# Local transformer of a twelve-stage kernel: queries scaled by their norms on GpSimd instead of the softmax exponents, with the sums of squares and the pieces of the feed-forward block moved

## The chip, the cores and the metric

The kernel runs on one core of a Trainium2 chip. The metric is the device time of one execution in microseconds; the median of three runs of the kernel before is 5602.67 us (5600.59 to 5613.93). The engines are named as in the profile: PE is TensorE's matrix multiply and PEld its weight load, DVE is VectorE, ACT is ScalarE, POOL is GpSimd, SP is SyncE, whose queue issues the DMAs here.

## The reference, cut to what matters

The reference is a chain of twelve blocks on x of 8 x 256 tokens, 128 wide. Blocks seven and nine are the same six-layer local transformer, `_L2_ffn_ref`, with the same weights; the change touches it alone. A layer of it is

```
q, k, v = split(shift_tokens(x) @ Wqkv)            # 16 heads of 64
q = l2norm(q) * q_scale ;  k = l2norm(k) * k_scale  # t / max(norm, 1e-12)
q, k = rotary with a scale for q and its inverse for k
sim  = (window of 32 queries) . (64 keys: window before and own) * 8
sim  = where(mask, -max, sim) ;  attn = softmax(sim) ;  out = attn @ v
x = out @ Wo + x
x = (a * gelu(gate)) @ W2 + b2 + x     # a, gate from layernorm(shift_tokens(x)) @ W1 + b1
```

The norm of a query is one number for each token and head. It may scale the query before the product with the keys, or the score row after it.

## The kernel before, in words

Tokens lie along the free axis in four groups of 512 (two sequences of 256), channels on the 128 partitions. The 16 heads are taken in four "quads" of four heads; in a quad's tiles of 128 x 2 x 512 the partitions hold two heads of 64 channels, and the index j holds the other two. A stage of the local transformer has 6 layers x 4 groups x 4 quads = 96 quads, so the two stages have 192.

`ffn2` (L1588) is a software pipeline written by hand. One pass of its loop, a *round*, works on four quads at once: q0 is projected, q1 gets its scores, q2 its exponentials and its product with the values, q3 is transposed back. Within these stages the calls go through `_Ordered` (L285), which ties each instruction of DVE, ACT, POOL and PE to the one issued before it on the same engine. So the order of calls in `ffn2` is the order on every engine.

What the steps of a round do:

- `quad_project` (L1315), for k and then for q: two 512-column products give `pp` in PSUM; ACT squares it into `l_sq`; DVE multiplies it by the cosines into `l_y`; DVE shuffles neighbouring partitions into `l_yr`; POOL multiplies that by the sines and adds it to `l_y`.
- `quad_norms` (L1345): four products with `hsum` add the squares of each head in one PSUM bank; ACT takes logarithm and exponential, which gives `l_rn`, the reciprocal norms times a constant, with k, q, k, q in four blocks of 32 rows; two DMAs on SP's queue bring the key rows to `l_rt`.
- `quad_pick` (L1357): eight small products with `hpick` turn the query rows of `l_rn` so that they lie as the score rows do; DVE bounds them by 1e12 into `l_rq`. Two DVE shuffles of 128 x 512 spread the rows of `l_rt` over the partitions, into a tile of the tag `l_sq`.
- `quad_keys` (L1375): one DVE scalar_tensor_tensor bounds that and multiplies the rotated keys by it, into `l_kp`.
- `quad_scores` (L1383): mask and 128 products of 64 x 32 give `sc`; DVE takes the row maximum `l_mx` and subtracts it, giving `l_e`; POOL multiplies `l_e` by `l_rq`.
- `quad_exp` (L1416): ACT's exponential of `l_e`. `quad_turn` (L1419): eight PE transposes `et`, which ACT copies to `l_at`. `quad_weigh` (L1429): 64 products in each of two halves `cx`, divided on DVE. `quad_back` and `quad_done`: eight transposes `ct`, copied by ACT to `l_ct`. `quad_values` (L1333): four products `vp`, copied by ACT to `l_v`, and two DMAs to `l_w`.

`pp`, `et`, `ct`, `cx`, `sc`, `vp` and `ge` share three PSUM tiles of two banks each. Which of them a step gets is settled when the program is built; it waits on the chip until that tile's last readers are done.

After the last quad of a group, `local_rest` (L1468) does the output projection and the feed-forward block in *pieces*; `piece` (L1583) runs the generator to its next `yield` at four places of each round. In what follows four rounds are told apart by the pieces in them. Round W: the output projection `wo_acc` in three pieces and the residual `x`, then the shifted copies `l_xs`. Round N: the layer norm, its first half (`acc`, `ln_c`, `ln_sq`) and its second (`acc`, `lv`, `ln_r`, `t`). Round G: the gated projections `ge`, `l_gl`, `l_ag` and two thirds of `w_acc`. Round X: the last third and the sum `x`. There are 48 such groups of four rounds.

Of the kernel before, what the change touches and what calls it, by code (L numbers as in the profile page):

```python
# [24 lines left out]
ALU = mybir.AluOpType  # L25
# [3 lines left out]
P = 128  # L29
B, S, D = 8, 256, 128  # L30
NB = 2
T = NB * S
# [6 lines left out]
WIN = 32  # L39
# [3 lines left out]
SH = 20.0  # L43
# [9 lines left out]
def _constants():  # L53

    f = np.float32
    p = np.arange(P)
    c = {}
    c["ident"] = np.eye(P, dtype=f)
    c["mean"] = np.full((P, P), 1.0 / P, f)
    c["ones"] = np.ones((P, P), f)  # L60
    c["iota"] = np.tile(np.arange(E, dtype=f), (P, 1))
    c["krow"] = (p % 32 == DH).astype(f)[:, None]
    c["eps"] = np.tile(
        np.array([1e-5, 2e-5, 2.0**-64, 0.5 * SH * math.log(2.0)], f), (P, 1)
    )
    blk = (p[:, None] // 64 == p[None, :] // 64).astype(f)
    c["blkm"] = blk / f(64)

    z = np.zeros((P, 32), f)
    z[:64, :16] = 1.0  # L70
    z[64:, 16:] = 1.0
    c["hsum"] = z
    z = np.zeros((P, 4), f)
    for n, r in enumerate((32, 96, 48, 112)):
        z[r, n] = 1.0
    c["hpick"] = z

    r = np.zeros((P, P), f)
    for m in range(P):
        if m % 2 == 0:  # L80
            r[m + 1, m] = -1.0
        else:
            r[m - 1, m] = 1.0
    c["rot2"] = r

    sel = np.zeros((P, 4, P), f)
    for g in range(4):
        for j in range(4):
            for d in range(DH):
                sel[DH * (4 * g + j) + d, g, 32 * j + d] = 1.0  # L90
    c["sel"] = sel.reshape(P, -1)


    lev = [np.eye(P, dtype=f)]
    for i in range(7):
        n = 2**i
        q = p // n
        lev.append(((q[:, None] % 2 == 0) & (q[None, :] == q[:, None] + 1)).astype(f))
    c["lev"] = np.concatenate(lev, 1)

    c["cq"] = np.where(p[None, :] > p[:, None], f(NEG), f(0))
    c["ck"] = np.where(p[:, None] > p[None, :], f(NEG), f(0))
    one9 = np.zeros((P, 32), f)
    one9[:, DH] = 1.0
    c["one9"] = one9


    i, key = np.arange(32), np.arange(64)
    ok = (key[None, :] >= i[:, None]) & (key[None, :] <= i[:, None] + WIN)
    m = np.zeros((2, 2, 32, 2, 64), f)  # L110
    m[:, 0] = np.where(ok, f(0), f(LNEG))[:, None, :]
    m[:, 1, :, 0, :WIN] = LNEG
    c["lmask"] = m.reshape(P, -1)
    m = np.zeros((2, 2, 32, 4, 32), f)
    m[:, 0] = np.eye(32, dtype=f)[:, None, :]
    m[:, 1, :, 0] = np.eye(32, dtype=f)
    c["lrow"] = m.reshape(P, -1)

    half = np.arange(0, 64, 2, dtype=f)
    inv_freq = f(1.0) / f(10000.0) ** (half / f(64))  # L120
    t = np.arange(S, dtype=f)
    fr = t[:, None] * inv_freq[None, :]
    fr = np.concatenate([fr, fr], -1).T
    base = (half + f(0.4 * 64)) / f(1.4 * 64)
    sc = base[None, :] ** ((t - f(S // 2)) / f(WIN // 2))[:, None]
    sc = np.concatenate([sc, sc], -1).T
    two = lambda a: np.concatenate([_partners(a.T).T] * 2, 0).astype(f)

    sgn = np.where(p[:64, None] < 32, f(-1), f(1))
    c["qcos"] = two(np.cos(fr) * sc * f(8.0))  # L130
    c["qsin"] = two(np.sin(fr) * sc * f(8.0) * sgn)
    c["kcos"] = two(np.cos(fr) * (f(1.0) / sc))
    c["ksin"] = two(np.sin(fr) * (f(1.0) / sc) * sgn)

    i = np.arange(DH // 2, dtype=f)
    th = np.power(f(10000.0), f(-2.0) * (i - f(1.0)) / f(DH))
    ang = t[:, None] * th[None, :]
    per = lambda a: np.tile(np.repeat(a.T, 2, axis=0), (NH, 1)).astype(f)
    c["rcos"] = per(np.cos(ang))
    c["rsin"] = per(np.sin(ang))  # L140

    groups = {
        "c1": ("ident", "mean", "ones", "iota", "krow", "eps"),
        "cs0": ("cq", "ck"),
        "cs1": ("lev", "blkm"),
        "cs2": ("hsum", "hpick", "lmask", "lrow", "qcos", "qsin", "kcos", "ksin"),
        "cs3": ("rot2", "sel", "ck", "one9", "rcos", "rsin"),
    }
    return {n: {k: c[k].astype(f) for k in ks} for n, ks in groups.items()}
# [159 lines left out]
class _Net:  # L309
# [1002 lines left out]
            out[k] = t.unsqueeze(1).to_broadcast([P, 4, S])  # L1312
        return out

    def quad_project(self, q, n):  # L1315

        nc = self.nc
        four = lambda a: a.rearrange("p j (b s) -> p (j b) s", b=NB)
        o = S if n == "k" else 0
        pp = self.two("pp")  # L1320
        for j in range(2):
            self.mm(pp[:, j, :], q.w[:, o + P * j : o + P * (j + 1)], q.xs)
        sq = self.work("l_sq", (P, 2, T), bufs=3)
        nc.scalar.activation(sq, pp, AF.Square)
        y = self.work("l_y" + n, (P, 2, T), bufs=2)
        nc.vector.tensor_tensor(four(y), four(pp), q.tab[n + "cos"], ALU.mult)
        yr = self.work("l_yr", (P, 2, T), bufs=2)
        nc.vector.stream_shuffle(yr, pp, [i ^ 1 for i in range(32)])
        nc.gpsimd.tensor_tensor(four(yr), four(yr), q.tab[n + "sin"], ALU.mult)
        nc.gpsimd.tensor_tensor(y, y, yr, ALU.add)  # L1330
        q.y[n], q.sq[n] = y, sq
# [10 lines left out]
        nc.sync.dma_start(w[:32, 1::2], v[96:, 0::2])  # L1342
        q.v = (w, v)

    def quad_norms(self, q):  # L1345


        nc = self.nc
        sp = self.ps()
        for s, (n, j) in enumerate((("k", 0), ("q", 0), ("k", 1), ("q", 1))):  # L1350
            self.mm(sp[32 * s : 32 * s + 32, :], self.get("hsum"), q.sq[n][:, j, :])
        q.rn = self.work("l_rn", bufs=2)
        self.rsqrt(q.rn, sp, 2, scale=2.0**SH, shift=3)
        for j in range(2):
            nc.sync.dma_start(self.rt[j::32], q.rn[64 * j : 64 * j + 32 : 8, :])

    def quad_pick(self, q):  # L1357


        nc = self.nc  # L1360
        tp = self.ps()[:, :16].rearrange("p (m r) -> p m r", r=4)
        for b in range(NB):
            for x in range(2):
                for c in range(2):
                    o = S * b + P * c + 64 * x
                    self.mm(tp[64 * c : 64 * c + 64, 2 * b + x, :], q.rn[:, o : o + 64], self.get("hpick"))
        q.rq = self.work("l_rq", (P, 16), bufs=2)
        nc.vector.tensor_scalar(
            q.rq.rearrange("p (r m) -> p r m", m=4), tp.rearrange("p m r -> p r m"), 1e12, None,
            ALU.min)  # L1370
        q.rk = self.work("l_sq", (P, 2, T), bufs=3)
        for j in range(2):
            nc.vector.stream_shuffle(q.rk[:, j, :], self.rt, [j] * 32)

    def quad_keys(self, q):  # L1375

        nc = self.nc
        q.kp = self.kp[q.n % len(self.kp)]
        nc.vector.scalar_tensor_tensor(
            q.kp[:, :, WIN:], q.rk.rearrange("p j (b s) -> p (j b) s", b=NB), 1e12,  # L1380
            q.y["k"].rearrange("p j (b s) -> p (j b) s", b=NB), ALU.min, ALU.mult)

    def quad_scores(self, q):  # L1383

        nc = self.nc
# [7 lines left out]
        for j in range(2):  # L1393
            for b in range(NB):
                for x in range(2):
                    o = S * j + P * b + 64 * x
# [9 lines left out]
        sl = lambda a: a.rearrange("p (n k) -> p n k", k=64)  # L1406
# [3 lines left out]
        nc.vector.tensor_reduce(mx, sv, AX.X, ALU.max)  # L1410
        e = self.work("l_e", (P, 2 * T), bufs=2)
        nc.vector.tensor_tensor(sl(e), sv, bc(mx), ALU.subtract)
        nc.gpsimd.tensor_tensor(sl(e), sl(e), bc(q.rq), ALU.mult)
        q.e = e

    def quad_exp(self, q):  # L1416
# [51 lines left out]
    def local_rest(self, u):  # L1468
# [5 lines left out]
        def project(cs):  # L1474
            for c in cs:
                self.mm(acc, u.w["wo"][:, c, :], u.ct[c // 2][:, c % 2, :], start=c == 0, stop=c == 7)
# [2 lines left out]
        yield False  # L1479
        project(range(3, 6))  # L1480
        yield False
        project(range(6, 8))
        u.x1 = self.new_x()
        nc.vector.tensor_tensor(u.x1, acc, self.ys[u.g], ALU.add)
        xs = self.shifted(u.x1)
        yield False

        yield False
        self.settle()
        norm = self.norm_parts(xs, gamma=self.get(f"F{i}_ln_g"), beta=self.get(f"F{i}_ln_b"),  # L1490
                               out=self.scratch("t", bufs=2), bank=self.bank1)
        next(norm)
        yield True
        yield True
        u.hn = yield from norm
# [92 lines left out]
    def ffn2(self):  # L1588
# [7 lines left out]
        while True:  # L1596
            q0 = next(gen, None)
            if not (q0 or q1 or q2 or q3 or left):
                break
            left = max(left - 1, 0)  # L1600
            if q1:
                self.quad_pick(q1)
            if q1:
                self.quad_keys(q1)
            if q0:
                self.quad_project(q0, "k")
                if not q0.n:
                    self.window_rows()
            if q2:
# [3 lines left out]
            self.piece(pieces)  # L1613
            if q2:
                self.quad_turn(q2)
            if q3:
                self.quad_back(q3)
                self.quad_done(q3)
                if q3.last:
                    pieces, left = self.local_rest(q3.unit), 4  # L1620
            if q2:
                self.quad_weigh(q2)
            self.piece(pieces, True)
            if q0:
                self.quad_norms(q0)
            self.piece(pieces)
            if q1:
                self.quad_scores(q1)
# [143 lines left out]
```

## Time and profile before

| What | Value |
|---|---|
| Median of three runs | 5602.67 us |
| Profiled execution, its own time | 5608.06 us |
| Span in its profile | 5606.2 us |
| Granted TensorE clock, mean | 0.974 |
| PE busy | 5052.7 us (90%) |
| DVE busy | 3506.1 us (63%) |
| ACT busy | 2461.2 us (44%) |
| POOL busy | 2340.9 us (42%) |
| Chain that ended last, by engine | PE 66%, DVE 20%, ACT 9%, issue 4%, POOL 1% |

Line 300 of the kernel is the helper in `_Ordered` that makes every call of the local transformer, so the groups of the profile are told apart by their tiles and not by lines. In a row "out<-in ... xN | busy, mean ns | idle before <-releaser" the last part is the idle time of the engine just before these instructions, and what ended most of it. `bank` is the one-bank tile that `hsum`'s and `hpick`'s products share with layer norms outside these stages. "issue" as a releaser means that the engine waited for nothing that the profile shows.

### The profile page before, as it was taken

What the parts mean: (1) busy time and instruction counts of PE and PEld (TensorE: products, weight loads), DVE (VectorE), ACT (ScalarE), POOL (GpSimd) and SP (SyncE); (2) the same over time, 40 slices, a digit from 0 to 9 for tenths busy, and PEclk for the clock granted to TensorE, in tenths of its full rate; (3) what the DMA queues carried; (4) which work ended last, traced back from release to release, by engine and by line L of the source; (5) the groups of instructions that cost most, each with busy time, mean ns of one, the idle gap of its engine ahead of it and who ended that gap; (6) DMA issues with size and microseconds to landing.
All of it is one profiled execution on the core that took longest, in us unless ns stands there. A gap on an engine that the chain in (4) does not pass through costs nothing.

```text
span 5606.2 us, 161762 instructions
## 1 busy us (share of the span) xinstructions
PE 5052.7 (90%) x73456; PEld 2970.4 (53%) x73456; DVE 3506.1 (63%) x5863; ACT 2461.2 (44%) x2947; POOL 2340.9 (42%) x1205
## 2 busy tenths in 40 slices
PE   9999997898999999989889899989899999899889
PEld 6755754455555555555444455555555555455446
DVE  4444446776766767676645667767667777645555
ACT  2233235444544444454434445544444554433342
POOL 0000012666665666666500666656566656501000
PEclk9999989999999999999989999999999999999899
DMA  1000000111111111111000011110111111000000
GB/s 66 1 1 1 1 1 22 30 35 37 36 40 33 39 34 41 34 35 34 26 23 1 26 38 37 35 38 28 45 30 44 31 38 34 26 34 1 1 1 8
DMA packets 58335, 149.56 MB, mean 27 GB/s; under 512 B 9649, under 2 KB 23858, under 8 KB 57394
## 3 DMA queue, kind: packets, MB, share of 16 engines
q1 hardware_dynamic: 57650, 139.21, 8.1%
q8 instruction: 578, 9.47, 0.7%
q14 instruction: 107, 0.88, 0.1%
HBM read 45.52 MB, written 1.05 MB: 8 GB/s over the span
## 4 chain that ended last, share of the span: by engine, by line
PE 66%; DVE 20%; ACT 9%; issue 4%; POOL 1%; DMA 0%; DVEq 0%; SPq 0%; ACTq 0%; POOLq 0%
PE mm L355 10%; PE bank L300 7%; PE e_o L355 6%; PE wo_acc L300 6%; PE sc L300 6%; PE pp L300 6%; PE vp L300 5%; PE ge L300 5%; DVE l_yr L300 4%; PE cx L300 4%; DVE l_yk L300 4%; PE ct L300 3%; PE ms L300 3%; DVE l_kp L300 2%; ACT l_ct L300 2%
## 5 line engine op out<-in xcount | busy, mean ns | idle before, releaser
L300 POOL TENSOR_TENSOR l_yr<-l_yr,l_ksin 128x1024 f32<-128x1024 f32 x192 | 456.2, 2376 | 1010.8 <-DVE l_yr L300 1010.8
L300 PE MATMUL pp<-l_xs,wqkv 128*128 128x512 f32 x1536 | 716.1, 609 | 5.2 <-DMA wqkv<-in_f_wqkv 3.6
L300 DVE TENSOR_REDUCE l_mx<-sc 128x16 f32<-128x1024 f32 x192 | 235.1, 1225 | 566.1 <-PE sc L300 566.1
L300 POOL TENSOR_TENSOR l_e<-l_e,l_rq 128x1024 f32<-128x1024 f32 x192 | 365.3, 1903 | 383.8 <-DVE l_e L300 357.8
L300 ACT ACTIVATE l_sq<-pp 128x1024 f32<-128x1024 f32 x384 | 391.1, 1018 | 279.6 <-PE pp L300 279.6
L300 DVE STREAM_SHUFFLE l_yr<-pp 128x1024 f32<-128x1024 f32 x384 | 505.3, 1316 | 0.0
L355 PE MATMUL mm<-x,m 128*128 128x512 f32 x1024 | 480.0, 609 | 1.2 <-ACT e_a L387 1.2
L300 ACT COPY l_v<-vp 128x1024 f32<-128x1024 f32 x192 | 194.3, 1012 | 611.8 <-PE vp L300 609.5
L300 POOL TENSOR_TENSOR l_yq<-l_yq,l_yr 128x1024 f32<-128x1024 f32 x192 | 454.9, 2369 | 15.1
L300 POOL TENSOR_TENSOR l_yk<-l_yk,l_yr 128x1024 f32<-128x1024 f32 x192 | 452.4, 2356 | 15.0
L300 POOL TENSOR_TENSOR l_yr<-l_yr,l_qsin 128x1024 f32<-128x1024 f32 x192 | 454.8, 2369 | 0.0
L300 PEld LDWEIGHTS pp<-l_xs,wqkv 128*128 128x128 f32 x1536 | 278.3, 191 | 290.3 <-issue 283.8
L300 PE MATMUL cx<-l_w,l_at 64*32 64x65 f32 x12288 | 326.2, 227 | 87.1 <-ACT l_ct L300 43.9
L355 PEld LDWEIGHTS e_o<-m,e_h 128*128 128x128 f32 x3072 | 363.0, 192 | 60.6 <-issue 60.1
L300 PE MATMUL vp<-wqkv,l_xs 128*128 128x256 f32 x1536 | 384.9, 393 | 6.2 <-issue 6.2
L355 PE MATMUL e_o<-m,e_h 128*128 128x128 f32 x3072 | 363.5, 275 | 0.0
L300 PE MATMUL wo_acc<-l_ct,wo 128*128 128x512 f32 x768 | 362.2, 605 | 0.0
L300 ACT ACTIVATE lv<-bank,sb_c 128x512 f32<-128x512 f32 x221 | 151.1, 684 | 478.0 <-PE bank L300 477.1
L300 PE MATMUL cx<-l_v,l_at 64*32 64x65 f32 x12288 | 334.1, 228 | 22.7 <-issue 22.7
L300 PEld LDWEIGHTS cx<-l_w,l_at 64*32 64x32 f32 x12288 | 259.2, 107 | 154.6 <-ACT l_ct L300 72.3
L300 PE MATMUL ct<-sb_c,l_cx 128*128 128x128 f32 x1536 | 206.6, 278 | 127.8 <-DVE l_yr L300 70.5
L300 PE MATMUL sc<-l_kp,l_yq 64*32 64x64 f32 x24576 | 297.9, 227 | 26.2 <-issue 25.5
(285 smaller groups left out, 9682.6 us busy)
## 6 DMA issues: line engine op xcount, KB each, us to landing
l_w<-l_v SPq DMA_DIRECT2D x192, 390.0 KB
wqkv<-in_f_wqkv SPq DMA_DIRECT2D x48, 384.0 KB
l_w<-l_v SPq DMA_DIRECT2D x192, 65.0 KB
wo<-in_f_wo SPq DMA_DIRECT2D x12, 512.0 KB
l_rt<-l_rn SPq DMA_DIRECT2D x384, 8.0 KB
m<-in_m_w SPq DMA_DIRECT2D x16, 256.0 KB
w<-in_f_w SPq DMA_DIRECT2D x12, 341.0 KB
w<-in_f_w SPq DMA_DIRECT2D x12, 192.0 KB
```

The source lines that it names most:

```text
L300: r = f(*args, **kw)
L355: self.nc.tensor.matmul(out, lhsT=lhsT, rhs=rhs, start=start, stop=stop)
```

## The change

`hpick`, its eight products, `l_rq` and POOL's multiplication of `l_e` are gone. Four DMAs instead of two bring the key rows and the query rows of `l_rn` to `l_rt`; four shuffles instead of two spread them. POOL bounds the queries' factors by 1e12 and multiplies the rotated queries `l_yq` by them, ahead of the scores. The tag `l_sq` has four buffers instead of three.

The order within a round changes in four places. The keys are scaled after the cosine product of the next quad's k instead of before it. The sums of squares stand between the transposes `et` and `ct` instead of after the products with the values, and their roots after the copy of `ct`. The pieces of a group begin at the first place of round W instead of the second. The first half of the layer norm stands at the first place of round N, between the projections and `quad_turn`, instead of the second place, after `quad_weigh`; the second half stays at the last place of round N, and the pieces of rounds G and X stay where they were.

```diff
-    c["hpick"] = z
...
+    def quad_project(self, q, n, q1=None):
...
+        sq = self.work("l_sq", (P, 2, T), bufs=4)
         nc.scalar.activation(sq, pp, AF.Square)
         y = self.work("l_y" + n, (P, 2, T), bufs=2)
         nc.vector.tensor_tensor(four(y), four(pp), q.tab[n + "cos"], ALU.mult)
+        if q1:
+            self.quad_keys(q1)
         yr = self.work("l_yr", (P, 2, T), bufs=2)
...
     def quad_norms(self, q):
         sp = self.ps()
         for s, (n, j) in enumerate((("k", 0), ("q", 0), ("k", 1), ("q", 1))):
             self.mm(sp[32 * s : 32 * s + 32, :], self.get("hsum"), q.sq[n][:, j, :])
+        q.sums = sp
+
+    def quad_roots(self, q):
+        nc = self.nc
         q.rn = self.work("l_rn", bufs=2)
+        self.rsqrt(q.rn, q.sums, 2, scale=2.0**SH, shift=3)
         for j in range(2):
+            for k in range(2):
+                at = 64 * j + 32 * k
+                nc.sync.dma_start(self.rt[2 * k + j :: 32], q.rn[at : at + 32 : 8, :])
+
+    def quad_spread(self, q):
+        nc = self.nc
+        q.r = {}
+        for k, n in ((1, "q"), (0, "k")):
+            r = q.r[n] = self.work("l_sq", (P, 2, T), bufs=4)
+            for j in range(2):
+                nc.vector.stream_shuffle(r[:, j, :], self.rt, [2 * k + j] * 32)
+        nc.gpsimd.tensor_scalar(q.r["q"], q.r["q"], 1e12, None, ALU.min)
+        nc.gpsimd.tensor_tensor(q.y["q"], q.y["q"], q.r["q"], ALU.mult)
...
-        nc.gpsimd.tensor_tensor(sl(e), sl(e), bc(q.rq), ALU.mult)
...                                              # local_rest
         project(range(3, 6))
         yield False
+        yield False
         project(range(6, 8))
         u.x1 = self.new_x()
         nc.vector.tensor_tensor(u.x1, acc, self.ys[u.g], ALU.add)
         xs = self.shifted(u.x1)
         yield False
 
-        yield False
         self.settle()
         norm = self.norm_parts(xs, ...)
         next(norm)
+        yield True
         yield True
         yield True
         u.hn = yield from norm
...                                              # ffn2
+            if q3 and q3.last:
+                pieces, left = self.local_rest(q3.unit), 4
             if q1:
-                self.quad_pick(q1)
-            if q1:
+                self.quad_spread(q1)
+            if q0:
+                self.quad_project(q0, "k", q1)
+            elif q1:
                 self.quad_keys(q1)
-            if q0:
-                self.quad_project(q0, "k")
...
             self.piece(pieces)
             if q2:
                 self.quad_turn(q2)
+            if q0:
+                self.quad_norms(q0)
             if q3:
                 self.quad_back(q3)
                 self.quad_done(q3)
-                if q3.last:
-                    pieces, left = self.local_rest(q3.unit), 4
+            if q0:
+                self.quad_roots(q0)
             if q2:
                 self.quad_weigh(q2)
             self.piece(pieces, True)
-            if q0:
-                self.quad_norms(q0)
             self.piece(pieces)
```

More of the change, by code (lines that the diff above doesn't have):

```diff
@@ L72, in _constants @@
     c["hsum"] = z
-    z = np.zeros((P, 4), f)
-    for n, r in enumerate((32, 96, 48, 112)):
-        z[r, n] = 1.0
-    c["hpick"] = z
     r = np.zeros((P, P), f)
@@ L145, in _constants @@
         "cs1": ("lev", "blkm"),
-        "cs2": ("hsum", "hpick", "lmask", "lrow", "qcos", "qsin", "kcos", "ksin"),
+        "cs2": ("hsum", "lmask", "lrow", "qcos", "qsin", "kcos", "ksin"),
         "cs3": ("rot2", "sel", "ck", "one9", "rcos", "rsin"),
@@ L1313, in local_tables @@
         return out
-    def quad_project(self, q, n):
+    def quad_project(self, q, n, q1=None):
         nc = self.nc
@@ L1322, in quad_project @@
             self.mm(pp[:, j, :], q.w[:, o + P * j : o + P * (j + 1)], q.xs)
-        sq = self.work("l_sq", (P, 2, T), bufs=3)
+        sq = self.work("l_sq", (P, 2, T), bufs=4)
         nc.scalar.activation(sq, pp, AF.Square)
@@ L1345, in quad_norms @@
     def quad_norms(self, q):
-        nc = self.nc
         sp = self.ps()
@@ L1351, in quad_norms @@
             self.mm(sp[32 * s : 32 * s + 32, :], self.get("hsum"), q.sq[n][:, j, :])
+        q.sums = sp
+    def quad_roots(self, q):
+        nc = self.nc
         q.rn = self.work("l_rn", bufs=2)
-        self.rsqrt(q.rn, sp, 2, scale=2.0**SH, shift=3)
+        self.rsqrt(q.rn, q.sums, 2, scale=2.0**SH, shift=3)
         for j in range(2):
-            nc.sync.dma_start(self.rt[j::32], q.rn[64 * j : 64 * j + 32 : 8, :])
-    def quad_pick(self, q):
+            for k in range(2):
+                at = 64 * j + 32 * k
+                nc.sync.dma_start(self.rt[2 * k + j :: 32], q.rn[at : at + 32 : 8, :])
+    def quad_spread(self, q):
         nc = self.nc
[L1361 to L1373, printed above, removed]
+        q.r = {}
[5 more added lines that the diff above has]
+        nc.gpsimd.tensor_tensor(q.y["q"], q.y["q"], q.r["q"], ALU.mult)
     def quad_keys(self, q):
@@ L1379, in quad_keys @@
         nc.vector.scalar_tensor_tensor(
-            q.kp[:, :, WIN:], q.rk.rearrange("p j (b s) -> p (j b) s", b=NB), 1e12,
+            q.kp[:, :, WIN:], q.r["k"].rearrange("p j (b s) -> p (j b) s", b=NB), 1e12,
             q.y["k"].rearrange("p j (b s) -> p (j b) s", b=NB), ALU.min, ALU.mult)
```

## The prediction

> **What bounds the kernel now.** The page's busy shares, the local stages by windows, groups by form, then four rounds of the timeline, engine by engine.
>
> ```profile
> span 5606.2 us, 161762 instructions
> PE 5052.7 (90%) x73456; PEld 2970.4 (53%) x73456; DVE 3506.1 (63%) x5863; ACT 2461.2 (44%) x2947; POOL 2340.9 (42%) x1205
> ```
> ```profile
> 1000.00:2900.00 1900.00, 1689.95 (x31089) 969.07 (x31090) 1289.40 (x1968) 912.97 (x1049) 1110.64 (x534) 0.98 0.12 35
> ```
> PE is busy 89% of a local stage, so a change counts by what it takes off PE and by the waits it leaves there. In all 192 rounds:
>
> ```profile
> L300 PE MATMUL bank<-sb_cs,l_rn 128*64 128x4 f32 x3072 | 122.8, 202 | 12.8 <-ACT lv L300 8.9 <-DVE ln_c L300 2.0 <-ACT ln_sq L300 0.7
> L300 PE MATMUL ct<-sb_c,l_cx 128*128 128x128 f32 x1536 | 206.6, 278 | 127.8 <-DVE l_yr L300 70.5 <-ACT l_at L300 57.3
> L300 POOL TENSOR_TENSOR l_e<-l_e,l_rq 128x1024 f32<-128x1024 f32 x192 | 365.3, 1903 | 383.8 <-DVE l_e L300 357.8 <-ACT l_gl L300 25.8
> L300 POOL COPY l_xs<-x 64x512 f32<-64x512 f32 x96 | 56.8, 616 | 22.9 <-DVE x L300 22.9
> ```
> `hpick`'s products cost PE about 0.6 us a round; before `ct` PE waits 127.8 us, for the k shuffle to free its PSUM tile or for `l_at`. Those are what the change could win. What it could lose shows in round N (2004.29 to 2021.14 us), on DVE, ACT and PE:
>
> ```profile
> 2004.39 0.69 DVE L300 TENSOR_TENSOR x<-wo_acc,x 128x512 f32<-128x512 f32 x1 [1.16 <-PE wo_acc L300]
> ...
> 2006.68 1.22 DVE L300 SCALAR_TENSOR_TENSOR l_kp<-l_sq,l_yk 128x1024 f32<-128x1024 f32 x1
> 2007.93 1.23 DVE L300 TENSOR_TENSOR l_yk<-pp,l_kcos 128x1024 f32<-128x1024 f32 x1
> ...
> 2011.42 1.33 DVE L300 STREAM_SHUFFLE l_yr<-pp 128x1024 f32<-128x1024 f32 x1
> ...
> 2014.66 0.69 DVE L300 TENSOR_TENSOR ln_c<-l_xs,acc 128x512 f32<-128x512 f32 x1
> ```
> ```profile
> 2010.16 1.01 ACT L300 COPY l_at<-et 128x1024 f32<-128x1024 f32 x1 [0.27 <-PE et L300]
> 2011.64 1.01 ACT L300 COPY l_ct<-ct 128x1024 f32<-128x1024 f32 x1 [0.47 <-PE ct L300]
> 2015.38 0.63 ACT L300 ACTIVATE ln_sq<-ln_c 128x512 f32<-128x512 f32 x1 [2.73 <-DVE ln_c L300]
> ```
> ACT runs in the order of the calls: `ln_sq` waits 2.73 us for `ln_c` and nothing passes it. And in round W (from 1981.32):
>
> ```profile
> 1982.88 1.91 POOL L300 TENSOR_TENSOR l_e<-l_e,l_rq 128x1024 f32<-128x1024 f32 x1
> ```
> ```profile
> 1984.13 1.74 DVE L300 SCALAR_TENSOR_TENSOR l_kp<-l_sq,l_yk 128x1024 f32<-128x1024 f32 x1
> ```
> `l_kp`, 1.22 us alone, took 1.74 here: it ended at 1985.87, 1.08 after the POOL instruction that ran when it was issued (end 1984.79). The longest POOL additions, 3.21 us against 2.37, are the mirror of it, with `l_kp` first. DVE instructions that read PSUM do not stretch.
>
> **The change part by part.** Lengths before, PE's start to start, unexplained "issue" pauses taken out: W 21.95 us (1981.32 to 2004.29 less 1.02), N 16.03 (to 2021.14 less 0.82), G 21.51 (to 2042.65), X 14.37 (to 2058.70 less 1.68). For after, 0 is the first `pp`. PE's pieces, from starts: the two `pp` 3.65, `et` 1.0, `hsum` 1.0, `ct` 1.0, each `cx` half 0.9, `sc` 1.74, `vp` 1.83, layer-norm products 1.0. On DVE: shuffles 0.63 apart, the last 0.84; `l_yk` and `l_kp` 1.14 apart, `l_yr` 1.2, `l_yq` 1.13.
>
> *Removed.* `hpick`: 0.57 a round (2021.14 to 2021.71), 2.3 a group, all on PE, taken by starting every round at `pp`. `l_rq` 0.17 of DVE. POOL's `l_e` product goes too, but the exponential hardly waits for it (13.5 us in its row): nothing.
>
> *Added on DVE.* Two shuffles, 1.26 a round, ahead of `l_yk`, `l_kp` and the k shuffle that frees `pp`. Without `l_rq`, DVE no longer waits for PE and starts as soon as the previous round lets it.
>
> *Added on POOL.* The bound (min) is not in the trace. Below: 0.92, half of the 2048-element memset (1.84 us), which reads nothing. Above: 1.90, the two-input `l_e` product. I take 1.23, twice the 512-element copy (one input, 0.616). Then the product, 2.37. The Trainium skill's "GPSIMD Engine Reference", section 3.1, gives 1.03 cycles an element for one input; that is an estimate of 0.88 us, and would make the sum some 50 us less. From the first two shuffles' end the two take 3.6 us; `l_kp` is issued 2.5 us after that end (1.47 for two shuffles, 1.14 for `l_yk`), so inside the product, every round. It then ends 1.08 after the product, about 1.1 us late, and the k shuffle, `l_yq`, q shuffle and all behind them with it. The skill's "SBUF — State Buffer", section Who interferes with whom, says of a DVE instruction with two SBUF inputs that the second to issue blocks until the first finishes. That speaks against the change; taken whole it would add 1.22 instead of the measured 1.08, another 20 us at most.
>
> *Moved: round N.* `x` ends at 0.8. Shuffles to 3.4, `l_yk`, `l_kp` issued 4.6; POOL: `l_xs` copies, min 2.3 to 3.5, product to 5.87; `l_kp` to 6.95, shuffles and `l_yq` to 10.65, `ln_c` 11.35, `ln_sq` 12.0. Only now comes `l_at` on ACT, to 13.0: behind the new wait stand `l_at`, `l_ct`, the roots and their DMAs, and PE needs `l_at` for `cx`. PE had 3.65 + `acc` 1.0 + `et` 1.0 + `hsum` 1.0 + `ct` 1.0, and `ct` waits for the k shuffle, 8.2; idle over 4 us in all. Then `cx` to 14.95, `sc` 16.7, `vp` 18.5, the second `acc` 19.5. **+3.5 us.**
>
> *Round G.* `t` ends at 2.85 (DVE waits for `ln_r`), shuffles 5.6, `l_kp` issued 6.7, product to 7.9, `l_kp` 8.98, k shuffle 10.25, q shuffle 12.65. `hsum` and `ct` are done by 7.5; one half of `cx` needs the k shuffle's tile: 10.35 to 12.15. `ge` needs a tile that the q shuffle frees, 12.75 to 16.4, then `sc`, `vp`, `ge`, `w_acc`: 23.45. **+1.95.**
>
> *Round X.* DVE free at 0.1; product to 5.1, `l_kp` 6.15, q shuffle 9.85. PE: `pp`, `w_acc` 0.86, `et`, `hsum`, `ct`, `cx` done by 9.4; `sc` at 10.0, `vp` ends 13.6. **-0.8.**
>
> *Round W.* The first piece of `wo_acc` (2.8) now fills PE while DVE works, and nothing waits: 3.65 + 2.8 + 3.0 + 1.8 + 2.8 + 1.74 + 1.83 + 1.8 = 19.4. **-2.55.**
>
> *At nothing.* Two more DMAs, 0.55 us each on SP's queue: `l_rn` to shuffle took 2.83 us at least with two, so 3.9 with four; round X, the tightest, has about 4.8, and loses what is missing if that cover goes. The `l_w` copies queued behind them on SP are read two rounds later. The fourth `l_sq` buffer keeps ACT from waiting.
>
> Sum: 3.5 + 1.95 - 0.8 - 2.55 = +2.1 a group, x 48 = **+101 us**. The profiled run, 5608.06, is 5.4 above the median of 5602.67; the sum goes onto the median: **5704 us**. Min at 0.92 takes 0.3 off N, G and X each: +1.2 a group, 5660. Min at 1.90 adds 0.7 to each: +4.2, 5804. If `ct` is given the k shuffle's tile in G and X, +0.4 each: +38.
>
> **The rivals.**
> - *The port stays free*: `l_kp` gets in ahead of POOL's product, because min lasts over 2.5 us or POOL comes late. Then N +2.3, G +0.85, X -0.9, W -2.55: -0.3 a group, 5588. Against it: POOL idled 3.5 us or more ahead of its sine products in these rounds. With it PE's "issue" pauses, 74 us in the rows of `cx`, `sc` and `vp`, may shrink too: down to 5514.
> - *ACT does not stop at `ln_sq`*: N then lasts 15.35 (`cx` after the k shuffle, `sc` after the q shuffle): -0.7 instead of +3.5, so -2.1 a group, 5502; and were DVE no limit either, `hpick`'s 2.28 and the 2.66 before `ct` (127.8/48) would give 5366. The 2.73 us wait above speaks against it.
> - *Slower than forecast*: min at 1.90 with `ct` late: +5.0 a group, 5843.
>
> **How the numbers follow.** Forecast 0.62; port free 0.16; ACT free 0.08; worse 0.14. The range 5580 to 5800 leaves out ACT free, the lower part of port free and most of worse, 2 in 10. A measurement here tells 0.3%, 17 us, from no change. Slower by more: 0.62 + 0.14 less 0.03 of the forecast's edge = 0.73. Faster: 0.08 + 0.10 of port free + 0.02 = 0.20. Same: 0.07.
>
> **What would show it.** In the profile after: `l_at` behind `ln_sq` in round N, and PE idle before `cx` by about 48 x 4 us with ACT `l_at` as releaser; `l_kp` at a mean near 2.3 us; `hpick`'s rows gone; round W shorter by 2 us or more; the wait before `ct` mostly gone. Wrong would be: `l_kp` at 1.3, or no idle time before `cx` in round N.

## The result: no difference, and the profile after

The changed kernel takes 5605.33 us (median of 14 runs), the kernel before 5605.81 us (14 runs): a ratio of 1.0001, 95% interval 0.9992 to 1.0010. The forecast was 5704 us, and its range began at 5580. The profiled execution took 5602.35 us. The helper that stood in line 300 stands in line 296 here. The page of after begins so:

```profile
span 5600.5 us, 156729 instructions
PE 4947.4 (88%) x70384; PEld 2956.5 (53%) x70384; DVE 3662.3 (65%) x6439; ACT 2439.0 (44%) x2947; POOL 3046.9 (54%) x1397
```

PE has 3072 products and 105 us of work less than before, and 100 us more idle time. POOL has 706 us more. In the windows view (length, busy time of PE, PEld, DVE, ACT and POOL with instruction counts, granted clock, DMA share, GB/s) the same stretch of a local stage shows PE at 1650 us instead of 1690, and a lower clock (0.98 before):

```profile
1000.00:2900.00 1900.00, 1650.10 (x29570) 969.30 (x29556) 1361.62 (x2246) 899.22 (x1048) 1450.82 (x625) 0.93 0.12 35
```

The next four rounds of the windows view are W, N, G and X of one group:

```profile
1899.79:1918.50 18.71, 18.71 (x315) 10.77 (x314) 13.36 (x22) 8.25 (x9) 17.11 (x7) 1.00 0.10 29
1918.50:1937.85 19.35, 14.46 (x304) 9.04 (x303) 13.89 (x23) 8.55 (x11) 16.08 (x8) 0.91 0.19 56
1937.85:1959.86 22.01, 18.89 (x315) 10.39 (x314) 15.78 (x26) 12.96 (x16) 14.95 (x6) 1.00 0.13 36
1959.86:1974.46 14.60, 12.77 (x301) 8.15 (x300) 12.61 (x23) 6.70 (x8) 12.91 (x5) 1.00 0.20 58
```

In W, PE never stops; in N it is idle for a quarter of the round. Over both stages, leaving out the first and last rounds of each, the mean lengths from one first `pp` to the next are:

| Round | before, us | after, us | difference | forecast |
|---|---|---|---|---|
| W | 22.04 | 18.81 | -3.23 | -2.55 |
| N | 16.33 | 19.99 | +3.66 | +3.5 |
| G | 21.86 | 22.89 | +1.03 | +1.95 |
| X | 15.48 | 14.68 | -0.80 | -0.8 |
| sum | 75.71 | 76.37 | +0.66 | +2.1 |

(Whole stages differ by less than the sum says: 1806.8 and 1783.9 us before, 1807.8 and 1782.8 after.) So what W wins N takes back. The list of waits (total us, times, longest; `PE cx <- ACT l_at` is idle time of PE before `cx` that ended with ACT's `l_at`) says who makes PE wait:

```profile
PE cx L296 <- ACT l_at L296: 152.4, 49, 3.3
PE cx L296 <- DVE l_yr L296: 94.7, 48, 2.9
PE sc L296 <- issue: 77.5, 83, 1.8
```

The first falls once in every round N, the second once in every round G. The timeline of ACT in the round N above shows the mechanism that was forecast: `ln_sq` waits 4.78 us for `ln_c`, and `l_at`, ready long before, goes behind it.

```profile
1922.59 1.01 ACT L296 ACTIVATE l_sq<-pp 128x1024 f32<-128x1024 f32 x1
1928.38 0.63 ACT L296 ACTIVATE ln_sq<-ln_c 128x512 f32<-128x512 f32 x1 [4.78 <-DVE ln_c L296]
1928.92 0.99 ACT L296 COPY l_at<-et 128x1024 f32<-128x1024 f32 x1
```

On PE, `cx` then starts 3.30 us late:

```profile
1925.60 1.07 PE L296 MATMUL ct<-sb_c,l_cx 128*128 128x128 f32 x8 [0.77 <-DVE l_yr L296]
1929.96 0.25 PE L296 MATMUL cx<-l_w,l_at 64*32 64x65 f32 x2 [3.30 <-ACT l_at L296]
```

What was forecast and did not come is in the groups by form, all 192 rounds:

```profile
L296 POOL TENSOR_SCALAR l_sq<-l_sq 128x1024 f32<-128x1024 f32 x192 | 535.5, 2789 | 553.4 <-DVE l_sq L296 553.1
L296 POOL TENSOR_TENSOR l_yq<-l_yq,l_sq 128x1024 f32<-128x1024 f32 x192 | 543.3, 2830 | 16.0
L296 DVE SCALAR_TENSOR_TENSOR l_kp<-l_sq,l_yk 128x1024 f32<-128x1024 f32 x192 | 239.7, 1248 | 0.2
```

POOL's bound takes 2.79 us, not 1.23, and `l_kp` takes 1.25 us, not 2.3: it is not held. It is POOL's product that stretches, from 2.37 to 2.83 us. In round N of the timeline, first POOL and then DVE:

```profile
1920.78 2.77 POOL L296 TENSOR_SCALAR l_sq<-l_sq 128x1024 f32<-128x1024 f32 x1 [0.17 <-DVE l_sq L296]
1923.63 2.81 POOL L296 TENSOR_TENSOR l_yq<-l_yq,l_sq 128x1024 f32<-128x1024 f32 x1
```
```profile
1922.99 1.22 DVE L296 SCALAR_TENSOR_TENSOR l_kp<-l_sq,l_yk 128x1024 f32<-128x1024 f32 x1
```

`l_kp` is issued while the bound still has 0.56 us to run, ends at 1924.21, and POOL's product, begun at 1923.63, ends 2.23 us after that. DVE comes first here.

### The profile page after: what moved, and what is told of

Same layout as the page of the kernel before. It is cut to its first block, busy times and chain, and to the rows that moved or that the text cites. A ratio compares the mean times of both kernels' runs of the same rounds, so it can differ in the third digit from the quotient of the medians.

```text
span 5600.5 us, 156729 instructions
## 1 busy us (share of the span) xinstructions
PE 4947.4 (88%) x70384; PEld 2956.5 (53%) x70384; DVE 3662.3 (65%) x6439; ACT 2439.0 (44%) x2947; POOL 3046.9 (54%) x1397
## 4 chain that ended last, share of the span: by engine, by line
PE 67%; DVE 18%; ACT 7%; issue 6%; POOL 2%; DMA 0%; DVEq 0%; ACTq 0%; SPq 0%; POOLq 0%
PE mm L351 10%; PE pp L296 7%; PE sc L296 7%; PE vp L296 7%; PE e_o L351 6%; PE wo_acc L296 6%; PE ge L296 5%; DVE l_sq L296 5%; DVE l_yr L296 5%; PE cx L296 4%; PE bank L296 3%; PE ms L296 3%; DVE l_kp L296 2%; PE w_acc L296 2%; DVE l_yq L296 2%
## 5 line engine op out<-in xcount | busy, mean ns | idle before, releaser
L296 POOL TENSOR_SCALAR l_sq<-l_sq 128x1024 f32<-128x1024 f32 x192 | 535.5, 2789 | 553.4 <-DVE l_sq L296 553.1
L296 PE MATMUL pp<-l_xs,wqkv 128*128 128x512 f32 x1536 | 695.0, 595 | 4.8 <-DMA wqkv<-in_f_wqkv 3.3
L296 POOL TENSOR_TENSOR l_yq<-l_yq,l_sq 128x1024 f32<-128x1024 f32 x192 | 543.3, 2830 | 16.0
L296 DVE STREAM_SHUFFLE l_sq<-l_rt 128x512 f32<-128x512 f32 x768 | 513.3, 743 | 0.0
L296 PEld LDWEIGHTS pp<-l_xs,wqkv 128*128 128x128 f32 x1536 | 293.4, 191 | 356.7 <-issue 328.5
L296 PEld LDWEIGHTS cx<-l_w,l_at 64*32 64x32 f32 x12288 | 280.9, 117 | 316.8 <-ACT l_at L296 166.2
L296 PE MATMUL sc<-l_kp,l_yq 64*32 64x64 f32 x24576 | 338.4, 240 | 92.4 <-issue 77.5
L296 PE MATMUL vp<-wqkv,l_xs 128*128 128x256 f32 x1536 | 408.2, 411 | 2.2 <-issue 2.1
L296 PEld LDWEIGHTS sc<-l_kp,l_yq 64*32 64x32 f32 x24576 | 287.6, 112 | 163.7 <-issue 143.1
```

The source lines that it names most:

```text
L296: r = f(*args, **kw)
```

## The experiments

Three theories stood after the result. *Order on ACT*: the change is worth some 3% but for the first half of the layer norm, whose new place costs that much again. *Port*: `l_kp` is free only because of what POOL runs at the moment of its issue. *Clock*: the idle time of round N lowers PE's clock, and that costs much of the loss.

### The layer norm's first half back at its place

```diff
 # after, local_rest
+        yield False
         self.settle()
...
         next(norm)
-        yield True
         yield True
         yield True
```

> The changed kernel with one thing undone: the first half of the layer norm is back at the second place of round N, after quad_weigh, so that on ACT the copy l_at no longer stands behind ln_sq. Theory A (the gain was given back in round N: ACT's order makes PE wait about 3.1 us for l_at before cx, and the clock granted to PE then falls to half for 5.7 us of that round): the wait is gone, cx follows ct, round N falls from 20.0 us to 15.1 to 15.6, the time at half clock in N goes from 5.7 us to near 0, and the kernel to 5365 to 5400 us. Theory B (the wait, but the clock is not tied to it): N loses 3.1 us, 5456 us, half clock as before. Theory C (DVE with its two more shuffles is the bound and the wait is only where its time shows): 5590 to 5605 us.

Measured: 5431.16 us, ratio to before 0.968 (0.9664 to 0.9696), between the times of theories A and B. N falls from 19.99 to 15.76 us, and the half clock, stretches in which the granted clock is 0.5, is gone from it (0.08 us a round). W and X stay at 18.78 and 14.67, and G is 0.4 us longer, at 23.27. ACT now runs `l_at` and `l_ct` ahead of `ln_sq`; a round N of this kernel's timeline:

```profile
1878.31 1.01 ACT L296 COPY l_at<-et 128x1024 f32<-128x1024 f32 x1 [0.27 <-PE et L296]
1880.50 1.01 ACT L296 COPY l_ct<-ct 128x1024 f32<-128x1024 f32 x1 [1.18 <-PE ct L296]
1884.55 0.63 ACT L296 ACTIVATE ln_sq<-ln_c 128x512 f32<-128x512 f32 x1 [1.69 <-DVE ln_c L296]
```

The `l_at` row is gone from the head of the list of waits. This version beats both kernels.

### Only the square moved

That edit moves a whole half of the layer norm: `acc` on PE, `ln_c` on DVE, `ln_sq` on ACT. Here `acc` and `ln_c` stay where the change put them, and `ln_sq` alone goes behind `l_at` and `l_ct`.

```diff
 # after, norm_parts and local_rest
-                   bank=None):
+                   bank=None, split=False):
...
         self.nc.vector.tensor_tensor(xc, x, m, ALU.subtract)
+        if split:
+            yield
         sq = tile("ln_sq")
...                                              # local_rest, with split=True in norm_parts' call
         next(norm)
         yield True
+        next(norm)
         yield True
```

> The changed kernel, its layer norm's first half still at the first place of round N (the mean's product on PE and ln_c on DVE as they are there), but the square ln_sq alone moved behind the copies l_at and l_ct on ACT. Theory A (the wait of round N is the order of two instructions on ACT): the 3.1 us before cx go, N falls from 20.0 us to 15.6 to 16.2, 5420 to 5455 us. Theory B (what hurts is the mean's product or ln_c at that place on PE and DVE): N stays above 18 us, 5530 us or more.

Measured: 5431.81 us, ratio 0.9688 (0.9668 to 0.9708), the same as with the whole half moved back. N is 15.70 us. All 174 us are the place of one instruction of 0.63 us in ACT's order.

### The parts one by one

Three versions lead from before to the version above. In the first only the spread is new: `hpick` out, four shuffles, POOL's bound and product, keys after the cosine product. In the second the pieces also start at the head of W. The third, above, moves the sums of squares and roots too.

```diff
 # the version above -> second: sums and roots late
-            if q0:
-                self.quad_norms(q0)
             if q3:
                 self.quad_back(q3)
                 self.quad_done(q3)
-            if q0:
-                self.quad_roots(q0)
...
             self.piece(pieces, True)
+            if q0:
+                self.quad_norms(q0)
+                self.quad_roots(q0)
 # second -> first: pieces late
-            if q3 and q3.last:
-                pieces, left = self.local_rest(q3.unit), 4
...
                 self.quad_done(q3)
+                if q3.last:
+                    pieces, left = self.local_rest(q3.unit), 4
...                                              # local_rest
         project(range(3, 6))
         yield False
-        yield False
```

> The kernel before with the change of its title alone: four shuffles, POOL's bound and product of the queries and the keys scaled after l_yk, instead of hpick and POOL's product of l_e; the sums of squares and all pieces stay where the kernel before has them. Theory A (the two more shuffles and the later k shuffle on DVE, for which ct and cx wait, take back most of hpick's 0.57 us a round): 5560 to 5620 us. Theory B (hpick's 109 us are won whole): 5490 to 5510 us.

> The kernel with the layer norm's first half back in its old place (5431 us), and the sums of squares and their roots too, after the products with the values as in the kernel before. It prices the moved sums. Theory A (between et and ct they fill time in which PE waits for the k shuffle or the copies): +1.0 us in G and X, up to 1.0 in N, nothing in W, less 0.5 us of issue pauses in X that the sums then part: 5500 to 5550 us. Theory B (PE has nothing to fill there): 5425 to 5450 us.

Measured: the spread alone 5605.81 us, ratio 1.0002 (0.9991 to 1.0012); with the pieces early 5528.56, ratio 0.9859 (0.9838 to 0.9881); with the sums moved 5431.16. So the steps are worth 0, -77 and -97 us, and the layer norm's +174. The spread alone wins nothing although `hpick` is gone, and its rows say why:

```profile
L296 PE MATMUL ct<-sb_c,l_cx 128*128 128x128 f32 x1536 | 216.4, 285 | 206.7 <-ACT l_at L296 204.0 <-DVE l_yr L296 2.7
```

The idle time before `ct` was 127.8 us before, 57.3 of it for `l_at`. Now `ct` waits in every round, 1.06 us from `et`'s end, about what the copy to `l_at` takes (1.01): in this kernel it gets the PSUM tile that `et` has just left, as before only in G. That adds 1.6 us a group, and `cx` in G waits 1.9 us for the k shuffle instead of 0.4, since DVE has two more shuffles; with small gains elsewhere the waits of a group grow by 2.2 us, which is `hpick`'s 2.3. The sums of squares between `et` and `ct` are 1.0 us of work for exactly this wait: in after, 53.6 us of idle time are left before `ct`.

The pieces were also moved alone, on the kernel before:

```diff
 # before, ffn2 and local_rest
+            if q3 and q3.last:
+                pieces, left = self.local_rest(q3.unit), 4
...
                 self.quad_done(q3)
-                if q3.last:
-                    pieces, left = self.local_rest(q3.unit), 4
...
         project(range(3, 6))
         yield False
+        yield False
```

> The kernel before with one part of the change alone: the pieces of a group begin at the first place of round W, so that the first wo_acc products stand between the projections and et; x, the layer norm and all else stay where the kernel before has them. Theory A (most of the gain of round W is this cover): W falls from 22.0 us by the 1.5 us of PE's waits before et and ct, N, G and X stay: 5530 us, within 20. Theory B (W gains from the missing products with hpick and the moved sums of squares): W falls by less than 0.5 us, 5585 to 5605 us.

Measured: 5567.27 us, ratio 0.9916 (0.9901 to 0.9931): -42 us, where the same move on top of the spread brings -77. That is neither theory: W falls by 0.9 us, to 21.11, and not by 1.5. The parts do not add up one by one.

### `hpick` put back

```diff
 # the best version (5431 us), quad_spread: hpick's eight products into a bank that nothing reads
...
+        tp = self.ps()[:, :16].rearrange("p (m r) -> p m r", r=4)
+        for b in range(NB):
+            for x in range(2):
+                for c in range(2):
+                    o = S * b + P * c + 64 * x
+                    self.mm(tp[64 * c : 64 * c + 64, 2 * b + x, :], q.rn[:, o : o + 64], self.get("hpick"))
...
```

> The kernel with the layer norm's first half back in its old place (5431 us), and the eight products with hpick of the kernel before put back on PE at the top of each round, their result unread. It prices what the change takes off PE. Theory A (PE bounds rounds W, N and X, and G waits for DVE anyway): +0.57 us in W, N and X, nothing in G: 82 us, 5510 us; were PE the bound in G too, 5540. Theory B (PE has idle time that hides them): 5431 to 5445 us.

Measured: 5553.77 us, ratio 0.9911 (0.9893 to 0.9929): 122.6 us more than without, and more than both sums of theory A. The row of these products before had 122.8 us busy, but the rounds show that the two numbers agree by chance. W is longer by 0.76 us, N by 0.52 and X by 1.68, and G is shorter by 0.54. In X something else has changed as well, as the row of `l_kp` in this kernel shows (its mean was 1.25 us without the products):

```profile
L300 DVE SCALAR_TENSOR_TENSOR l_kp<-l_sq,l_yk 128x1024 f32<-128x1024 f32 x192 | 322.7, 1681 | 0.2
```

In X the cosine product `l_yk`, which stands ahead of `l_kp` on DVE, now waits 1.0 us instead of 0.25. So `l_kp` is issued on average 0.58 us after the end of POOL's bound, where it was issued 0.17 us before it, and meets POOL's product: in 46 of the 48 rounds X it is stretched, and its mean there is 2.86 us. In W and N, where `l_kp` still goes ahead of the product on average, the products cost 0.5 to 0.8 us a round. How much of X's 1.68 us is PE's work and how much the meeting was not parted.

### POOL without its bound, and with half of it

The first leaves the bound out, the second applies it to half of the factors only.

```diff
 # after, quad_spread
-        nc.gpsimd.tensor_scalar(q.r["q"], q.r["q"], 1e12, None, ALU.min)
 # or
+        half = q.r["q"][:, 0, :]
+        nc.gpsimd.tensor_scalar(half, half, 1e12, None, ALU.min)
```

> The changed kernel without POOL's bound of the queries' factors at 1e12 (left out: the bound, which only a query of norm zero would need). POOL's product of the queries then starts as soon as the two query shuffles are done, and l_kp is issued while it runs. Theory A (l_kp escapes the port only because the bound takes 2.79 us and lets it go first): l_kp grows from 1.25 to 2.2 or 2.3 us in every round, the k and q shuffles end 1 us later, N and G grow by about 1 us each: 5680 to 5720 us. Theory B (POOL is what is late, 2.8 us less of it helps): l_kp stays at 1.25 us and the time at or under 5605 us.

> The changed kernel with POOL's bound at 1e12 on one half (j = 0) of the queries' factors alone; the other half is left unbounded. The bound should take 1.4 us instead of 2.79, so that POOL's product of the queries runs from 1.4 to 3.8 us after the query shuffles, and l_kp, issued 2.5 us after them, meets it in the middle, as the prediction had it for every round. Theory A (the port blocks, and the prediction failed in the bound's price alone): l_kp 2.2 to 2.4 us instead of 1.25, N and G longer by about 1.2 us each, 5660 to 5730 us. Theory B (such a meeting costs less than the kernel before showed, or DVE has slack there): l_kp longer, time within 5600 to 5625 us.

Measured: without the bound 5624.07 us, ratio 1.0029 (1.0017 to 1.0041); with half of it 5805.43, ratio 1.0355 (1.0338 to 1.0372). The first is neither theory: `l_kp` takes 1.32 us. The expectation used wrong arithmetic: the product, 2.39 us here, starts with the first two shuffles' end and is nearly over when `l_kp` is issued (in 139 of 192 rounds it still runs, with 0.24 us left on average). Why this kernel is 0.3% slower was not followed. The second goes the way of theory A, but beyond its 5730 us. It puts the product where the prediction had it; the rows of this second kernel:

```profile
L296 DVE SCALAR_TENSOR_TENSOR l_kp<-l_sq,l_yk 128x1024 f32<-128x1024 f32 x192 | 440.6, 2295 | 0.2
L296 POOL TENSOR_SCALAR l_sq<-l_sq 128x512 f32<-128x512 f32 x192 | 290.1, 1511 | 611.3 <-DVE l_sq L296 611.2
```

and one round of its timeline, POOL and then DVE:

```profile
1992.41 1.49 POOL L296 TENSOR_SCALAR l_sq<-l_sq 128x512 f32<-128x512 f32 x1 [8.07 <-DVE l_sq L296]
1993.98 2.37 POOL L296 TENSOR_TENSOR l_yq<-l_yq,l_sq 128x1024 f32<-128x1024 f32 x1
```
```profile
1995.31 2.12 DVE L296 SCALAR_TENSOR_TENSOR l_kp<-l_sq,l_yk 128x1024 f32<-128x1024 f32 x1
```

POOL's product ends at 1996.35, `l_kp` at 1997.43, which is 1.08 us later, as in the row of before that the prediction read. It costs 200 us against after. Half the work on POOL makes the kernel 3.6% slower.

### Keys ahead of the cosine product

Whether the full bound holds `l_kp` or was only nearly over is told apart by issuing `l_kp` 1.1 us earlier.

```diff
 # the best version, ffn2
-            if q0:
-                self.quad_project(q0, "k", q1)
-            elif q1:
+            if q1:
                 self.quad_keys(q1)
+            if q0:
+                self.quad_project(q0, "k")
```

> The version with the layer norm's first half back at its old place, in which moreover the keys are scaled ahead of the cosine product, as before the change. The keys' product l_kp is then issued some 1.1 us after POOL's bound starts (the bound lasts 2.78 us, so 1.7 us of it are left), where it was issued 0.2 to 0.6 us before the bound's end. Theory A, POOL's one-input bound does not hold DVE's product with two SBUF inputs at all: l_kp stays at 1.2 to 1.3 us, POOL's product behind the bound starts after l_kp has ended and is back at 2.4 us instead of 2.83, and the time is that of the version it is built on, 5431 us, within 15 us. Theory B, the bound holds such an instruction as POOL's two-input product does, and it only escaped because it was issued when the bound's reads were over: l_kp lasts 2.8 us or more (1.7 us left, and 1.1 after that), everything behind it on DVE is 1.6 us late in every round, and the time rises by 100 us or more.

Measured: 5469.98 us, ratio 0.9762 (0.9746 to 0.9778). In 185 of 192 rounds `l_kp` is issued inside the bound, on average 1.46 us before its end, and lasts 1.23 us. A round of this kernel's timeline, POOL and then DVE:

```profile
1912.48 2.77 POOL L296 TENSOR_SCALAR l_sq<-l_sq 128x1024 f32<-128x1024 f32 x1 [2.97 <-DVE l_sq L296]
1915.34 2.37 POOL L296 TENSOR_TENSOR l_yq<-l_yq,l_sq 128x1024 f32<-128x1024 f32 x1
```
```profile
1913.83 1.22 DVE L296 SCALAR_TENSOR_TENSOR l_kp<-l_sq,l_yk 128x1024 f32<-128x1024 f32 x1
```

Theory A: neither instruction stretches, though `l_kp` lies wholly inside the bound. In the other 7 rounds `l_kp` met a two-input POOL addition (`l_yq` plus `l_yr`) and lasted 3.20 us on average. The Trainium skill, "SBUF — State Buffer", section Who interferes with whom, says that a DVE instruction with two SBUF inputs contends with a GpSimd instruction that reads SBUF; for POOL's two-input product and addition the runs agree, for this one-input instruction they do not. The time missed theory A's 15 us: it is 39 above the best version, with X 0.4 us longer. The rows show DVE idle for 21.6 us before `l_kp`, 0.11 us a round, which was 0.2 us in all with the cosine product between the shuffle and `l_kp`. In X PE now waits 0.28 us a round before `ct` for the k shuffle, which it did not before; that is about a third of the 39. The rest was not followed.

### PE filled in round N

```diff
 # after, quad_back: three 128x512 products into ct's tile, overwritten by the transposes
+        if q.n % 4 == 0:
+            for j in (0, 1, 0):
+                self.mm(tp[:, j, :], self.get("ident"), q.unit.xs)
...                                              # ffn2 keeps xs in the unit for it
```

> The changed kernel with work added: in round N three products of 128 x 512 into the PSUM tile of ct, ahead of the transposes that overwrite it, about 2.8 us of PE, so that PE is busy while it would wait for l_at. Nothing else moves. If the half clock follows from the idle time before cx (theory A), the time at half clock in N goes from 5.7 us to near 0, sc and vp there get shorter, and N falls by 2 to 2.8 us although PE does more: 5470 to 5510 us. If the clock is lowered for another reason (B), N stays at 20.0 us or grows a little: 5605 to 5620 us.

Measured: 5595.45 us, ratio 0.9975 (0.9963 to 0.9986), between the two theories. In after the clock is halved for 5.69 us of an average round N, in stretches that begin between 3.5 us before the end of the 3.3 us wait and 1 us after it; with the filler for 0.47 us, and the wait before `cx` shrinks to 0.7 us at most. N falls by 0.43 us only, from 19.99 to 19.56. This kernel's waits tell where the rest went:

```profile
PE sc L296 <- issue: 119.4, 85, 2.1
PE cx L296 <- DVE l_yr L296: 92.2, 48, 2.9
...
PE cx L296 <- ACT l_at L296: 31.1, 47, 0.7
```

The pauses before `sc` that no profiled event explains grew from 77.5 to 119.4 us, in N from 0.69 to 1.48 us a round. The kernel with only the square moved shows the same exchange: 0.24 us at half clock and 1.19 us of these pauses a round N. So removing the half clock brings back about 10 of the 174 us. What it would bring without the pauses, and what they are, stays open.

### Two attempts to better the best version

The last third of `w_acc` between `cx` and `sc` in X, to break up the 64 x 32 products; and the spread at the end of the round before, with `l_kp` first in the round.

```diff
 # local_rest
+        yield False
         second(2)
 # or ffn2
             if q1:
-                self.quad_spread(q1)
-            if q0:
-                self.quad_project(q0, "k", q1)
-            elif q1:
                 self.quad_keys(q1)
             if q0:
+                self.quad_project(q0, "k")
...
                 self.quad_values(q0)
+                self.quad_spread(q0)
```

> The kernel with the layer norm's first half back in its old place (5431 us), and in round X the last third of w_acc, 0.86 us of PE, moved from the first place to the second, between cx and sc. Theory A (PE's issue pauses, 0.95 us a round X in the products sc, come from cx and sc, some 500 instructions, standing next to each other, and a long product between them lets the supply catch up): the pauses in X fall to 0.4 us or less, X from 14.7 to 14.1, 5400 us. Theory B (the pauses belong to something else): they stay, 5431 us.

> The kernel with the layer norm's first half back in its old place (5431 us), and the spreading of the norms (four shuffles, POOL's bound and product) moved to the end of the round before, ahead of its last piece, with l_kp ahead of l_yk as in the kernel before. In round G the shuffles, 2.7 us of DVE, then lie in the time in which DVE waits for ln_r. Theory A (round G's 23.3 us is DVE's chain from t through four shuffles to the k and q shuffles, for which cx and ge wait, with the clock at half for 2.9 us behind it): cx's 2.1 us of waiting in G goes, the half clock with it, G falls to 20.5 to 21.5 us: 5290 to 5350 us. Theory B (the l_rt DMAs land too late, or l_kp meets POOL's product, and DVE waits there instead): 5420 us or more.

Measured: 5446.21 us, ratio 0.9713 (0.9694 to 0.9732), and 5555.86, ratio 0.9910 (0.9889 to 0.9932); neither beats 5431. In the first the pauses before `sc` in X fall from 1.06 to 0.15 us a round, as its theory A had it, but X keeps its length, 14.67 us: `et` now waits 0.34 us for the exponential and a bank 0.13 us for `x`. That is about half of what the pauses gave; the rest was not followed. The second is theory B: `l_kp` meets POOL's product in 34 of 46 rounds G and takes 3.37 to 3.39 us there, and G grows to 24.72 us. N grows too, to 17.14 us, with PE waiting 1.9 us before `et` for the exponential. Twice in this kernel `l_kp` meets POOL's copies of `l_xs` instead, which have one input. Once, POOL and then DVE:

```profile
2673.40 1.83 POOL L296 COPY l_xs<-x 64x512 f32<-64x512 f32 x2
```
```profile
2674.68 1.63 DVE L296 SCALAR_TENSOR_TENSOR l_kp<-l_sq,l_yk 128x1024 f32<-128x1024 f32 x1
```

The copies end at 2675.23 and `l_kp` at 2676.31, again 1.08 us later. So having one input is not in itself what makes the bound harmless.

## Why the prediction was wrong

**The failed step is one price.** It stands under "Added on POOL": the bound was taken at 1.23 us between 0.92 and 1.90, from a memset, a copy and a product, and it takes 2.79. The upper end rested on an assumption that no row showed, that one input costs less than two. The estimate of 0.88 us from the Trainium skill's "GPSIMD Engine Reference", section 3.1, is further off still. From that price followed "so inside the product, every round", and with it the forecast. With 2.79 us, `l_kp` is issued before the product starts, which is the rival "The port stays free" with its condition "min lasts over 2.5 us"; it gave 5588 and had a chance of 0.16. That 5588 lies so near the measured 5605 is partly luck: against that rival's own rounds W came out 0.68 us shorter and N 1.36 us longer.

**What stood behind that step was right, and would have cost more.** With the half bound the product lies where the prediction put it: `l_kp` at 2.295 us (forecast near 2.3), ending 1.08 us after the product. The time is then +200 us. The forecast was +101 for a bound of 1.23 us; half the bound takes 1.51, for which the prediction's own scale (0.28 us more in N, G and X each) gives some +140. N is 21.59 us, +5.26 to before instead of +3.8 by that scale, and G 24.43, +2.57 instead of +2.2.

**ACT's order was right, by the right mechanism.** `l_at` stands behind `ln_sq`, and PE is idle before `cx` in every round N, 3.3 us a round where about 4 was forecast. N's +3.66 is even nearer to the forecast's +3.5 than to the +2.3 of the rival that came true, but for a mixed reason. In the trace `cx` starts 11.53 us after `pp` on average, not at 13.0, because `l_kp` is not held and the bound does not delay it; behind it, PE needs 8.46 us to the round's end instead of the 6.5 summed up. "Issue" pauses are 0.7 us of that, and half clock falls into it; with the square moved and the half clock gone this part still takes 8.20 us, with more pauses. So this term of the sum for N was some 2 us short, and it hid in the total what the missing stretch of `l_kp` saved there. The rival "ACT does not stop at `ln_sq`" is, with one instruction moved, the kernel of 5431 us; it was put at 5502.

**W was undersized, X right, G as in the rival.** W wins 3.23, not 2.55: PE runs without a stop, as forecast, but its pieces take 18.8 us and not the 19.4 summed up. X is at -0.80 as forecast, although `l_kp` is not held there either: the rival's X, -0.9, shows that the forecast for X hardly hung on it. G is at +1.03, near the rival's +0.85.

**Removing `hpick`** was put at 0.57 us a round, on PE and so on the path. Its return to the best version costs 0.76 us in W and 0.52 in N, which is near that; in X and G it moves DVE and POOL as well, so that the total of 122.6 us is no price of PE's work alone. In the spread alone the waits behind it took all of the gain. The wait before `ct` was to be mostly gone, and fell from 127.8 to 53.6 us.

So the change came out at nothing because a gain of 174 us, from the earlier pieces and the moved sums, met a loss of 174 us from one ACT instruction. The prediction knew both terms of this, with other sizes; what it added was a third, the stretch of `l_kp`, that did not occur.

## What to carry to other kernels

When work is moved ahead on an engine that runs in order, look at what it waits for and at what stands behind it: here 0.63 us of work put one place too early cost 3%. A price without a row of its own needs wide bounds, and when a branch of the forecast hangs on it, both branches should be carried with their time; a cheaper instruction ahead of a transfer of a shared resource can make a kernel slower, by shifting which of two engines comes first. Take the parts of a change apart on the chip before judging it: one that measures as nothing may hold a large gain and an equal loss. And look at the rounds of every such run: a total that equals the expected price, as with `hpick` put back, may hold something else.

## What the runs showed of the hardware

- POOL's one-input TENSOR_SCALAR (minimum with a constant, float) takes 2.79 us for 128x1024 and 1.51 us for 128x512; the two-input product of 128x1024 takes 2.37 us.
- That one-input instruction does not hold DVE's product with two SBUF inputs (1.23 us, issued 1.46 us before its end, 185 rounds); POOL's two-input product does (2.295 us on average in the kernel with half a bound), and twice a one-input COPY of POOL did (end 1.08 us after the copy's). Why they differ no run here shows.
- A wait of some 3.3 us on PE goes with half clock, 5.69 us in an average round N; filling the wait takes the half clock to 0.47 us, but here recovered 0.43 us a round. Rounds G of after, with a wait of 2.1 us before `cx`, have 2.44 us of half clock on average, and only about half of them have any.
- PE pauses without a visible cause before `sc`, where the many small products of `cx` and `sc` follow each other: 77.5 us in after, 119.4 with the filler. A product of 0.86 us put between `cx` and `sc` took them from 1.06 to 0.15 us a round X. What they are is open.
